# Attention in a macaron block: the softmax row sums of the last four heads taken by matmuls with ones instead of ScalarE's accumulator

## The chip, the core and the metric

The kernel runs on one core of a Trainium2 chip. A core has five engines that run side by side and meet through semaphores: TensorE (PE, matmuls into PSUM), VectorE (DVE), ScalarE (ACT), GpSimd (POOL) and SyncE (SP, which only issues transfers). The metric is the device time of one execution in microseconds (us); a time of a kernel is the median of its runs.

## The reference

The block is a mixture-of-experts layer, an attention layer and the same mixture-of-experts layer again, each added to its input, over x of shape 8 x 1024 x 512 in float32. Only the attention part concerns the change. It has 16 heads of 32 columns:

```python
q = (x @ Wq.T + bq).reshape(B, L, H, hd)      # B, L, H, hd = 8, 1024, 16, 32
k = (x @ Wk.T + bk).reshape(B, L, H, hd)
v = (x @ Wv.T + bv).reshape(B, L, H, hd)
q = _apply_rope(q, cos, sin); k = _apply_rope(k, cos, sin)
scores = jnp.einsum('bqhd,bkhd->bhqk', q, k) / np.sqrt(hd)
attn = jax.nn.softmax(scores, axis=-1)
out = jnp.einsum('bhqk,bkhd->bqhd', attn, v).reshape(B, L, D)
return out @ Wo.T + bo
```

The softmax needs, for every query and head, the maximum of 1024 scores and the sum of their exponentials.

## The kernel before

The work is cut into 32 units: 8 batches b times 4 column blocks c, and a unit holds four heads. The first and the last part of the program are the expert layers; in between, `Attention.run` calls `stage` for every unit and once more at the end. A stage has 16 slots, written out by hand in program order for PE, ACT, DVE and POOL, so no scheduler moves anything: each engine runs its own list in that order, and waits only for data and for free buffers.

A stage does two things at once. It takes a unit's scores for the first time with queries in the rows ("top": matmuls of L1838, 128 queries by 1024 keys for two head pairs in a slot), finds each row's maximum (`tensor_reduce`, L1846, on VectorE), and forms the exponentials of these scores with the accumulator on (L1850, on ScalarE): the exponentials themselves are thrown away, only their sum per row is kept, in `total0` and `total2`. And for the unit before it ("sum") it forms the scores again with keys in the rows: the negative maxima come in as a rank-3 product of bfloat16 pieces (L1802), then the scores (L1809) are added in PSUM, and ScalarE's exponentials (L1816 and L1818) are the weights `pr`. In every even slot `weighed` multiplies the weights of the two slots before with the values (L1906: eight products, which the trace shows as 16 matmul records, of 128 keys by 32 columns for 512 queries; the four heads fill four column strips of the array) and VectorE adds the result to `oT` (L1912 the first time, L1915 later). After four such groups a half of the queries is done, and `oT` is multiplied with the inverse of the sums (L1918, by GpSimd; by VectorE for the very last).

The inverses come from `rows_of`, a small task that starts after each half of a unit's tops: GpSimd splits the maxima in bfloat16 pieces (L1863, L1865), VectorE takes the reciprocals of the sums (L1870, two of 128x8), PE transposes pieces and inverses (L1877, L1880), VectorE copies them out (L1884, L1886), and SyncE writes the inverses to DRAM (L1888) and reads them back spread over 32 partitions a head (L1892) into the tile `d`.

PSUM has eight banks of 512 columns, taken as four pairs with turning roles. In a slot with both parts, pairs b and d hold the sums' scores, a and c the tops'; then b's place becomes the next a, a's the next d, and d's the next b, while c stays c. So PE can write a slot's L1802 into the old a only when the old a has been read for the last time. What an even slot's L1906 or a group of other matmuls needs is put in pair b as soon as it has been read; in the stage without tops it goes to pair c.

Other matmuls fill the slots: projections of the next unit (L1213), values and outputs (L1232). The output of a finished half of a batch is four groups, each a product of four `oT` tiles with the output weights, added to the row x by VectorE (L1946, L1948). The last stage with tops has only one output group, in slots 0 and 1. The stage after it has no tops: it sums the last unit and carries the output of the last batch's first half in its slots 9, 11, 13 and 15. Then `ending` does what is left: the last weighed sums, the output of the second half (L1349, L1360, L1364), the routing of the last tokens to the experts (L272 to L341, among them L296), their ranking, and the scatters into the expert table (L307, by GpSimd), before the second expert layer begins with a gather from that table. `step` hands out the small VectorE tasks of such routing by an estimated credit per slot; `product` hands out small PE tasks where a bank is spare.

Of the kernel before, what the change touches and what calls it, by code (L numbers as in the profile page):

```python
# [13 lines left out]
F32 = mybir.dt.float32  # L14
I32 = mybir.dt.int32
BF16 = mybir.dt.bfloat16
AF = mybir.ActivationFunctionType
ALU = mybir.AluOpType
# [4 lines left out]
P = 128  # L23
NHEAD = 16
HD = 32
# [1029 lines left out]
class Attention:  # L1055
# [13 lines left out]
    def __init__(  # L1069
# [23 lines left out]

        self.passed = 0

    def start(self, task, rank=2):
# [145 lines left out]
    def stage(self, top, sum_, fill, begin, whole=False):  # L1244

        self.loose = []
        for i in range(self.SLOTS):  # L1250
            self.now += 1
            self.scores(i, top, sum_)
            for rank, task in begin.get(i, ()):
                self.start(task, rank)
            b, d, a, c = self.roles
            side = self.pair(b if top and sum_ else d if top else c)
            weigh = i % 2 == 0 and self.behind
            first, second = (side[:, (i + n) % 2, :] for n in range(2))
            self.spare = [first]
            if weigh:  # L1260
                self.spare = []
                self.weighed(first)
            if sum_:
                self.behind.append((*sum_, i, self.prs))
            if self.half:
                assert i not in fill
                self.group(P, 512, second, False)
            elif i in fill:
                self.half = fill[i]()
                if whole:  # L1270
                    self.group(0, 512, second, False)
                else:
                    self.group(0, P, second, bool(weigh))
            if not (top and sum_ or self.half or i in fill):
                self.spare.append(second)
            for _ in list(self.spare):
                self.product()
            self.step(3.0 if not top else 1.2 if i % 2 else 2.0)
            self.roles = [d, a, b, c]
        self.spare = None  # L1280

    def last_sums(self):
        if self.behind:
            self.weighed(self.take())

    def run(self):
        nc, tc = self.nc, self.tc
# [497 lines left out]
    def scores(self, i, top, sum_):  # L1785


        nc, pool = self.nc, self.pool
        heads = [slice(h * HD, (h + 1) * HD) for h in range(4)]
        at_b, at_d, at_a, at_c = self.roles  # L1790
        self.prs = {}
        if sum_:
            q, k = self.qk[sum_][0], self.qk[sum_][1]
            n, t = divmod(i, self.LT)
            row = self.mrow[(*sum_, n)]
            sbs = [(2, self.pair(at_b)), (0, self.pair(at_d))]
            if not top:
                sbs = [(2, self.pair(at_d)), (0, self.pair(at_b))]
            for pair, sb in sbs:
                for h in range(2):  # L1800
                    at = (pair + h) * HD
                    nc.tensor.matmul(  # L1802
                        sb[:, h, :], self.ones16[at : at + 3, :], row[at : at + 3, :],
                        start=True, stop=False,
                    )
            for pair, sb in sbs:
                for h in range(2):
                    at = heads[pair + h]
                    nc.tensor.matmul(  # L1809
                        sb[:, h, :], k[at, t * P : (t + 1) * P], q[at, n * 512 : (n + 1) * 512],  # L1810
                        start=False, stop=True,
                    )
                self.prs[pair] = pr = pool.tile([P, 2, 512], F32, tag="pr", bufs=6, name="pr")
                if pair and top:
                    for h in range(2):
                        nc.scalar.activation(pr[:, h, :], sb[:, h, :], AF.Exp)  # L1816
                else:
                    nc.scalar.activation(pr, sb, AF.Exp)  # L1818
        if top:
            qa, ka = self.qk[top][0], self.qk[top][1]  # L1820
            j, odd = divmod(i, 2)
            g, j = divmod(j, 4)
            assert {(*top, 0, g), (*top, 1, 0), (*top, 1, 1)} <= self.done, (top, i, self.tasks)
            if i % 8 == 0:
                self.held = {
                    name: pool.tile([P, 4, n], F32, tag=name, name=name)
                    for name, n in (("nm", 4), ("total0", 2), ("total2", 2))
                }
                self.until[g] = self.now + 8
            nm, se = self.held["nm"], {pair: self.held[f"total{pair}"] for pair in (0, 2)}  # L1830
            at_q = slice(j * P, (j + 1) * P)
            own, swapped, cross = qa[:, g * 512 : (g + 1) * 512], self.swapped[(*top, g)], self.cross[top]
            tops = [(0, self.pair(at_a)), (2, self.pair(at_c))]
            for pair, sa in tops:
                for m in range(2):
                    at = heads[pair + m]
                    here = m == odd
                    nc.tensor.matmul(  # L1838
                        sa[:, m, :], (own if here else swapped)[at, at_q],
                        ka[at, m * 512 : (m + 1) * 512] if here else cross[at, :],  # L1840
                        start=True, stop=True,
                    )
            for pair, sa in tops:
                h = pair + odd
                flat = sa.rearrange("p m k -> p (m k)")
                nc.vector.tensor_reduce(nm[:, j, h : h + 1], flat, AX.X, ALU.max, negate=True)  # L1846
            for pair, sa in tops:
                h = pair + odd
                flat = sa.rearrange("p m k -> p (m k)")
                nc.scalar.activation(  # L1850
                    flat, flat, AF.Exp, bias=nm[:, j, h : h + 1], accum_out=se[pair][:, j, odd : odd + 1],
                )
            if i % 8 == 7:
                self.start(self.rows_of(*top, g, nm, se), rank=0)

    def rows_of(self, b, c, g, nm, se):


        nc, pool = self.nc, self.pool
        yield WAIT, 1  # L1860
        p, m = self.pieces[g], nm
        for i in range(3):
            nc.gpsimd.tensor_copy(p[:, :, :, i], m)  # L1863
            if i < 2:
                nc.gpsimd.tensor_tensor(nm, m, p[:, :, :, i], ALU.subtract)  # L1865
        yield WAIT, 1
        yield DVE, 0.3
        over = pool.tile([P, 4, 4], F32, tag="sum", name="sum")
        for pair, total in se.items():
            nc.vector.reciprocal(over[:, :, pair : pair + 2], total)  # L1870
        yield WAIT, 1
        yield PE, 0.7

        bank = self.psum.tile([P, 512], F32, name="tp16")
        tp = bank[:, 0:256].bitcast(BF16).rearrange("p (t q) -> p t q", t=4)
        for t in range(4):
            nc.tensor.transpose(  # L1877
                tp[:, t, :], p[:, t, :, :].rearrange("p h d -> p (h d)"), self.ident16
            )
        nc.tensor.transpose(  # L1880
            bank[0:16, 256:384], over.rearrange("p t h -> p (t h)"), self.s.ident
        )
        self.mrow[b, c, g] = row = pool.tile([P, 512], BF16, tag="mrow", name="mrow")
        nc.vector.tensor_copy(row, tp.rearrange("p t q -> p (t q)"))  # L1884
        few = pool.tile([16, P], F32, tag="few", bufs=1, name="few")
        nc.vector.tensor_copy(few, bank[0:16, 256:384])  # L1886
        kept = self.inverse[g]
        nc.sync.dma_start(kept.rearrange("h (t q) -> t h q", q=P), few)  # L1888
        yield WAIT, 8
        self.over[b, c, g] = d = pool.tile([P, 512], F32, tag="d", name="d")  # L1890
        for h in range(4):
            nc.sync.dma_start(  # L1892
                d[h * HD : (h + 1) * HD, :], kept[h : h + 1, :].partition_broadcast(HD)
            )

    def weighed(self, po):


        nc, LT, behind = self.nc, self.LT, self.behind
# [3 lines left out]
        for j, (_, _, _, prs) in enumerate(behind):  # L1903
            for h in range(4):
                at = h * HD
                nc.tensor.matmul(  # L1906
                    po[at : at + HD, :], self.v[b][t + j][:, c * P + at : c * P + at + HD],
                    prs[h // 2 * 2][:, h % 2, :], start=(j == 0), stop=(j == len(behind) - 1),
                )
        if t == 0:  # L1910
            self.oT[b, c, n] = oT = self.pool.tile([P, 512], F32, tag="oT", bufs=10, name="oT")
            nc.vector.tensor_copy(oT, po)  # L1912
            return
# [215 lines left out]
```

## Time and profile before

| | |
|---|---|
| time, median of 3 runs (lowest to highest) | 4379.53 us (4377.94 to 4381.6) |
| the profiled execution's own time | 4387.33 us |
| its span, first to last instruction | 4385.5 us |
| TensorE busy in the span | 4253.2 us (97%), mean granted clock 0.985 |
| ScalarE busy | 2617.3 us (60%) |
| VectorE busy | 2593.8 us (59%) |
| GpSimd busy | 1402.3 us (32%) |

Durations come from the profiled execution, which is one run; its time is compared with the median where a forecast needs it. Matmuls are pipelined and the profile models their ends, so a busy TensorE is not TensorE at its peak. The granted clock is the share of full speed that the throttle gives TensorE. The attention stages lie between 925 and 3590 us of the span; the last stage with tops takes 3441 to 3525 us, the stage without tops 3525 to 3582.

### The profile page before, as it was taken

To read this page: it belongs to the slowest core of one execution; us is meant where nothing else is said; L and a number is where in the kernel's file an instruction comes from. 1 tells how busy PE (TensorE), PEld (TensorE's weight loads), DVE (VectorE), ACT (ScalarE), POOL (GpSimd) and SP (SyncE) were. 2 spreads that over 40 slices of the span, in tenths; PEclk is the share of its full clock that TensorE was granted. 3 is DMA by queue.
4 is the path that set the end of the run, shared out by engine and by line. 5 is a ranking of instruction groups with operands and counts; after the bars stand their busy time and mean duration, and the time that the engine had idled before them with its cause. 6 is when DMAs were issued, how large, how long until landed. Compare 5 with 4: busy or idle time off the path is not lost.

```text
span 4385.5 us, 84431 instructions
## 1 busy us (share of the span) xinstructions
PE 4253.2 (97%) x32371; PEld 2412.4 (55%) x32371; DVE 2593.8 (59%) x4942; ACT 2617.3 (60%) x4325; POOL 1402.3 (32%) x1640
## 2 busy tenths in 40 slices
PE   8899999989999999999999999999999879999999
PEld 6566777744444444444444444444444335667777
DVE  8434433356666876876776877777766634334333
ACT  6112122137888888888888888888888842122221
POOL 7344444321232232232232232332232213333332
PEclk9999999988999999999999999999999999999999
DMA  4656666531112212222212212312212116566664
GB/s 156 221 187 192 211 209 230 182 110 50 43 47 64 80 46 66 77 47 65 80 46 63 80 46 65 81 45 66 79 39 62 35 43 210 185 206 205 215 222 164
DMA packets 310835, 495.59 MB, mean 113 GB/s; under 512 B 65049, under 2 KB 99235, under 8 KB 310418
## 3 DMA queue, kind: packets, MB, share of 16 engines
q1 hardware_dynamic: 269698, 412.06, 30.9%
q0 software_dynamic: 39776, 76.77, 5.4%
q8 instruction: 257, 4.21, 0.4%
q14 instruction: 160, 1.31, 0.1%
q10 hardware_dynamic: 944, 1.23, 0.1%
HBM read 379.85 MB, written 87.93 MB: 107 GB/s over the span
## 4 chain that ended last, share of the span: by engine, by line
PE 90%; DVE 4%; issue 2%; ACT 1%; DMA 1%; POOL 1%; SPq 0%; POOLq 0%; DVEq 0%; ACTq 0%
PE s L1232 11%; PE s L1838 11%; PE s L1213 11%; PE gp L969 10%; PE s L1809 10%; PE s L1906 10%; PE up L969 10%; PE yp L1015 9%; PE s L1802 4%; PE tp L957 2%; PE yp L1023 1%; ACT s L1850 1%; DVE nm L1846 1%; DVE st L164 1%; PE s L207 1%
## 5 line engine op out<-in xcount | busy, mean ns | idle before, releaser
L1846 DVE TENSOR_REDUCE nm<-s 128x1 f32<-128x1024 f32 x1024 | 1205.7, 1219 | 556.2 <-PE s L1838 555.0
L1850 ACT ACTIVATE s<-s,nm 128x1024 f32<-128x1024 f32 x1024 | 1114.3, 1088 | 158.4 <-DVE nm L1846 147.6
L974 ACT ACTIVATE sg<-gp 128x320 f32<-128x320 f32 (+7 forms) x256 | 99.7, 389 | 1062.0 <-PE gp L969 1008.3
L1816 ACT ACTIVATE pr<-s 128x512 f32<-128x512 f32 x992 | 538.3, 594 | 242.6 <-PE s L1809 240.4
L1744 POOL TENSOR_TENSOR raw<-raw,a 128x512 f32<-128x512 f32 x125 | 158.8, 1270 | 1374.0 <-DMA rot<-raw 1202.4
L1838 PE MATMUL s<-cross,swapped 32*128 32x512 f32 x2048 | 569.7, 615 | 7.5 <-DMA cross<-k 3.1
L1838 PE MATMUL s<-k,q 32*128 32x512 f32 x2048 | 567.4, 611 | 0.0
L1818 ACT ACTIVATE pr<-s 128x1024 f32<-128x1024 f32 x528 | 541.9, 1030 | 22.4 <-PE s L1809 22.4
L1809 PE MATMUL s<-q,k 32*128 32x512 f32 x4096 | 551.6, 598 | 0.5 <-issue 0.3
L1213 PE MATMUL s<-hT,wqk 128*32 128x128 f32 (+2 forms) x4864 | 502.1, 323 | 9.1 <-ACT pr L1816 5.2
L1906 PE MATMUL s<-pr,big 128*32 128x512 f32 x4096 | 495.2, 601 | 0.7 <-DVE lg L1948 0.7
L969 PE MATMUL gp<-bT,wg 128*128 128x272 f32 (+7 forms) x1984 | 488.7, 389 | 0.0
L969 PE MATMUL up<-bT,wu 128*128 128x272 f32 (+7 forms) x1984 | 484.9, 387 | 0.0
L1213 PEld LDWEIGHTS s<-hT,wqk 128*32 128x32 f32 (+1 forms) x4864 | 295.5, 127 | 287.7 <-ACT pr L1816 96.9
L1015 PE MATMUL yp<-wd,a 128*128 128x512 f32 x992 | 445.9, 592 | 0.0
L969 PEld LDWEIGHTS gp<-bT,wg 128*128 128x128 f32 x1984 | 371.6, 190 | 87.4 <-issue 21.4
L969 PEld LDWEIGHTS up<-bT,wu 128*128 128x128 f32 x1984 | 374.4, 190 | 70.3
L996 DVE TENSOR_TENSOR a<-sg,up 128x320 f32<-128x320 f32 (+7 forms) x256 | 110.8, 433 | 490.8 <-PE up L969 395.9
L1906 PEld LDWEIGHTS s<-pr,big 128*32 128x32 f32 x4096 | 107.3, 109 | 357.6 <-ACT pr L1816 194.1
L1838 PEld LDWEIGHTS s<-k,q 32*128 32x128 f32 x2048 | 243.8, 186 | 105.2 <-DVE raw L1685 40.2
L1019 DVE SCALAR_TENSOR_TENSOR ys<-yp,gates,x 128x512 f32<-128x512 f32 x128 | 96.1, 751 | 336.9 <-PE yp L1015 336.9
L1838 PEld LDWEIGHTS s<-cross,swapped 32*128 32x128 f32 x2048 | 227.4, 186 | 120.4 <-DVE raw L1685 21.9
(310 smaller groups left out, 5388.7 us busy)
## 6 DMA issues: line engine op xcount, KB each, us to landing
wg<-in_w_gate SPq DMA_DIRECT2D x62, 1024.0 KB
wu<-in_w_up SPq DMA_DIRECT2D x62, 1024.0 KB
wd<-in_w_down SPq DMA_DIRECT2D x62, 1024.0 KB
rot<-raw SPq DMA_DIRECT2D x1000, 32.0 KB
all<-in_x SPq DMA_DIRECT2D x32, 512.0 KB
xt<-first_rows SPq DMA_DIRECT2D x64, 256.0 KB
swapped<-q SPq DMA_DIRECT2D x256, 64.0 KB
d<-inverse SPq DMA_DIRECT2D x256, 64.0 KB
```

The source lines that it names most:

```text
L969: nc.tensor.matmul(acc, w[:, k, f * P : (f + 1) * P], to.bT[:, k, 0:width], start=(k == 0), stop=(k == s.KD - 1),)
L1015: nc.tensor.matmul(yp, a[:, f, i * P : (i + 1) * P], wd[:, f, :], start=(f == 0), stop=(f == KF - 1),)
L1213: self.nc.tensor.matmul(acc[a : a + w, lo:hi], one[:, a : a + w], two[:, lo:hi], start=(i == 0), stop=(i == len(terms) - 1),)
L1232: self.nc.tensor.matmul(bank[a : a + w, 0 : to - at], one[:, a : a + w], two[:, at:to], start=(i == 0), stop=(i == len(terms) - 1),)
L1802: nc.tensor.matmul(sb[:, h, :], self.ones16[at : at + 3, :], row[at : at + 3, :], start=True, stop=False,)
L1809: nc.tensor.matmul(sb[:, h, :], k[at, t * P : (t + 1) * P], q[at, n * 512 : (n + 1) * 512], start=False, stop=True,)
L1816: nc.scalar.activation(pr[:, h, :], sb[:, h, :], AF.Exp)
L1818: nc.scalar.activation(pr, sb, AF.Exp)
L1838: nc.tensor.matmul(sa[:, m, :], (own if here else swapped)[at, at_q], ka[at, m * 512 : (m + 1) * 512] if here else cross[at, :], start=Tru ...
L1846: nc.vector.tensor_reduce(nm[:, j, h : h + 1], flat, AX.X, ALU.max, negate=True)
L1850: nc.scalar.activation(flat, flat, AF.Exp, bias=nm[:, j, h : h + 1], accum_out=se[pair][:, j, odd : odd + 1],)
L1906: nc.tensor.matmul(po[at : at + HD, :], self.v[b][t + j][:, c * P + at : c * P + at + HD], prs[h // 2 * 2][:, h % 2, :], start=(j == 0), s ...
```

## The change

For the units in `self.plain`, which holds only the last one (batch 7, column block 3), the accumulating exponentials are left out. In the stage without tops, every even slot that calls `weighed` for this unit now also multiplies the same weights `pr` with a block of ones, of the same shape as the block of values, into the second bank of the pair, `pd`. Each row of the result holds the sum over 256 keys, already spread over the 32 partitions of its head, so neither transposes nor transfers are needed. VectorE copies or adds `pd` into `d` and, after a half's last group, takes the reciprocal of all of `d` (128x512); these stand in its order ahead of the copy or add into `oT`. `rows_of` then only splits, transposes and copies the maxima. A slot that uses the second bank hands out no small PE task. Everything else is the same.

```diff
@@ __init__
+        self.plain = {(B - 1, s.KD - 1)}
@@ stage
             weigh = i % 2 == 0 and self.behind
+            both = bool(weigh) and self.behind[0][:2] in self.plain
...
-                self.weighed(first)
+                self.weighed(first, second if both else None)
...
-            if not (top and sum_ or self.half or i in fill):
+            if not (top and sum_ or self.half or i in fill or both):
                 self.spare.append(second)
@@ last_sums
-            self.weighed(self.take())
+            both = self.behind[0][:2] in self.plain
+            self.weighed(self.take(), self.take() if both else None)
@@ scores
+            if top in self.plain:
+                se = {}
...
             for pair, sa in tops:
+                if not se:
+                    continue
                 h = pair + odd
                 flat = sa.rearrange("p m k -> p (m k)")
                 nc.scalar.activation(
@@ rows_of
         yield WAIT, 1
+        if not se:
+            yield PE, 0.5
+            bank = self.psum.tile([P, 512], F32, name="tp16")
+            tp = bank[:, 0:256].bitcast(BF16).rearrange("p (t q) -> p t q", t=4)
+            for t in range(4):
+                nc.tensor.transpose(
+                    tp[:, t, :], p[:, t, :, :].rearrange("p h d -> p (h d)"), self.ident16
+                )
+            self.mrow[b, c, g] = row = pool.tile([P, 512], BF16, tag="mrow", name="mrow")
+            nc.vector.tensor_copy(row, tp.rearrange("p t q -> p (t q)"))
+            return
@@ weighed
-    def weighed(self, po):
+    def weighed(self, po, pd=None):
...
+        if pd is not None:
+            for j, (_, _, _, prs) in enumerate(behind):
+                for h in range(4):
+                    at = h * HD
+                    nc.tensor.matmul(
+                        pd[at : at + HD, :], self.s.ones[:, at : at + HD],
+                        prs[h // 2 * 2][:, h % 2, :], start=(j == 0), stop=(j == len(behind) - 1),
+                    )
+            if t == 0:
+                self.over[b, c, n] = self.pool.tile([P, 512], F32, tag="d", name="d")
+                nc.vector.tensor_copy(self.over[b, c, n], pd)
+            else:
+                d = self.over[b, c, n]
+                nc.vector.tensor_tensor(d, d, pd, ALU.add)
+                if t + len(behind) == LT:
+                    nc.vector.reciprocal(d, d)
```

More of the change, by code (lines that the diff above doesn't have):

```diff
@@ L1261, in stage @@
                 self.spare = []
-                self.weighed(first)
+                self.weighed(first, second if both else None)
             if sum_:
                 self.behind.append((*sum_, i, self.prs))
+            assert not (both and (self.half or i in fill))
             if self.half:
```

## The prediction

> **What bounds the kernel now.** I read the page first: the shares of the chain that ended last, and the costliest groups.
>
> ```profile
> PE 90%; DVE 4%; issue 2%; ACT 1%; DMA 1%; POOL 1%; SPq 0%; POOLq 0%; DVEq 0%; ACTq 0%
> L1850 ACT ACTIVATE s<-s,nm 128x1024 f32<-128x1024 f32 x1024 | 1114.3, 1088 | 158.4 <-DVE nm L1846 147.6
> ```
>
> Over the whole run TensorE (PE) sets the end, and ScalarE's accumulating exponentials (L1850) are 1% of the chain. That average hides the one place where the change acts: the last of 32 stages that form row maxima, and the stage behind it that only sums. So I asked for busy times by stretch: one ordinary stage, the part of the last maximum stage that has no projections or outputs left in it (slots 2 to 15), and the start of the sum stage.
>
> ```profile
> 3365.00:3445.00 80.00, 80.00 (x808) 38.22 (x804) 59.02 (x104) 69.65 (x115) 23.53 (x28) 1.00 0.22 58
> 3451.60:3525.40 73.80, 56.01 (x411) 21.64 (x411) 45.86 (x73) 60.39 (x100) 7.35 (x11) 0.91 0.04 12
> 3527.00:3570.00 43.00, 39.74 (x316) 15.64 (x313) 9.12 (x21) 25.48 (x27) 3.70 (x7) 0.98 0.06 19
> ```
>
> Columns are length, then busy PE, weight loads, VectorE (DVE), ScalarE (ACT), GpSimd, then the granted clock. In an ordinary stage PE is never idle, so freed ScalarE time there would be worth nothing. In slots 2 to 15 of the last maximum stage PE idles 18 of 74 us and gets a clock of 0.91; ScalarE is the busiest. The chain of waits shows how a slot turns there, and, below the dots, two slots of the sum stage.
>
> ```profile
> 3467.21 0.39 PE s L1802 x2
> 3467.60 0.86 PE s L1809 x8
> 3468.46 0.87 PE s L1838 x6
> 3469.36 1.24 DVE nm L1846
> ...
> 3470.62 1.21 ACT s L1850 x2
> ...
> 3471.87 0.39 PE s L1802 x2
> ...
> 3544.63 1.85 PE s L1906 x16
> 3546.49 0.33 PE s L1802 x4
> 3546.81 0.94 PE s L1809 x8
> 3547.78 1.03 ACT pr L1818
> ...
> 3548.85 0.39 PE s L1802 x2
> ```
>
> The first part is a loop of 4.66 us per slot: scores, maximum, exponential, and only then may PE write the next scores into that PSUM pair. The second is 5.47 us for two slots: PE works all but about 1.0 us, which it waits for one exponential.
>
> **What the change does, part by part.** The order of instructions after the change holds what the diff says: 32 L1850 and their accumulator reads go, eight groups of 16 matmul records with ones come in right behind the L1906 groups of the sum stage and its end, and VectorE gets eight 128x512 copies or adds and two 128x512 reciprocals. GpSimd's order stays. Ten transfers of inverses leave SP's queue; they are off the chain, worth nothing.
>
> *Gain in slots 2 to 15.* Fourteen turns of 4.66 us are 65.2; the stretch took 73.7 (3451.66 to 3525.39). The other 8.5 are four windows of 3.4 us at half clock (in each a slot's L1809 took 1.71 for 0.86, its L1838 some 0.7 more: 1.5 each, 6.0), one PE halt at 3507.55 (L1809 2.15 for 0.86: 1.3), and VectorE's routing work (about 1.2). Without L1850 the pair is free when its maximum ends. An odd slot then takes 0.39 + 0.86 + 0.87 + 0.03 + 1.24 + 0.04 = 3.45. In an even slot the weighed sums (L1906) come between: PE needs 1.85 + 0.33 + 0.86 + 0.87 = 3.9, but VectorE needs 1.07 from the start of L1838 to its first maximum, 2.35 for the two, 0.69 for the add from PSUM that frees the next bank: 4.1. Seven pairs are 7 x 7.55 = 52.9. VectorE is the next bound: per slot only about 1.1 us of it is free, and the routing lumps (3.0 us in slot 8 to 9, 1.4 in slot 4, others smaller) overflow that by about 3.5 together. Half-rate windows followed PE idleness: the 3.4 us before each were at most 62% busy. Odd slots now idle about 1.1 us of 3.45, so I keep two of four windows (3.0) and the halt (1.3). The stretch is then 52.9 + 3.5 + 3.0 + 1.3 = 60.7, a gain of 13.0. Slots 0 and 1 carry an output group each and are PE-bound; nothing there.
>
> *Loss in the sum stage.* The products with ones have the shape and count of L1906, so 1.86 us each. They stand between an even slot's scores and the odd slot's scores, while PE's 1.0 us wait comes after the odd scores; nothing hides them. Seven in the stage: 13.0. VectorE's copies and adds of the new sums are free where no output group follows, since it is 80% idle there.
>
> *The reciprocal 128x512* is in no row. The rows for its price:
>
> ```profile
> L1870 DVE RECIPROCAL sum<-total 128x8 f32<-128x8 f32 x128 | 16.7, 172 | 0.0
> ...
> L300 DVE RECIPROCAL se<-se 128x4 f32<-128x4 f32 x16 | 2.8, 178 | 0.6
> L1563 DVE RECIPROCAL sd<-rstd 128x4 f32<-128x4 f32 x16 | 2.6, 169 | 0.0
> L510 DVE RECIPROCAL se<-se 128x8 f32<-128x8 f32 x7 | 1.4, 203 | 0.2
> ```
>
> L300 and L510 both run alone after a wait, so their difference is a slope: 25 ns for 4 columns, 6.25 ns a column, 0.18 + 508 x 0.00625 = 3.35 us. L1870 runs pipelined and its 172 ns for 8 columns is no more than 4 columns cost; by that a 128x512 would cost what an add does, 0.66. From L1563 (169) to L510 the step is 34 ns for 4 columns, 8.5 each, 0.17 + 508 x 0.0085 = 4.5. So the ends are 0.66 and 4.5. I take 3.35, since an instruction that waits for its operand, as here, is like L300 and L510.
>
> The Trainium skill speaks against a cheap one: VectorE: DVE Perf Modes (section "First, the fixed hardware budget") says that reciprocal is an iterative divide with a repeat count of 8. If that means 8 cycles a column at the 0.96 GHz of its specifications, one costs an estimated 4.4 us; by the page the sum below would be 2 us worse.
>
> *Where it bites.* (1) Slot 8 ends the first half's sums. Its reciprocal stands in VectorE's queue ahead of the add into oT, and slot 9's output group (L1232) writes the bank which that add frees, so output, later scores and exponentials queue behind it. From the end of the products: 0.07 + 0.69 + 0.05 + 3.35 + 0.05 + 0.69 = 4.9; PE comes to L1232 after 1.1. Stall 3.8. GpSimd's multiply (1.27) ends before the last terms need it. (2) The output groups of slots 11, 13, 15 and the transposes of slot 3 wait for two VectorE operations in place of one: 1.45 against 1.1, 0.35 each, 1.4. (3) The end is one VectorE queue:
>
> ```profile
> 3582.57 1.92 PE L1906 MATMUL s<-pr,big 128*32 128x512 f32 x16 [0.72 <-DVE lg L1948]
> 3585.30 0.66 DVE L1915 TENSOR_TENSOR oT<-oT,s 128x512 f32<-128x512 f32 x1
> ...
> 3586.61 0.37 DVE L296 TENSOR_TENSOR lg<-s,oh 128x128 f32<-128x128 f32 x1
> ```
>
> The last products end at 3584.49 + 1.86 = 3586.35; then add 0.69, reciprocal 3.35, and L1915 ends at 3591.2, not 3585.96: 5.2. Behind it wait routing, ranking, the table's scatters and the second expert phase; VectorE has no pause before 3590, so all 5.2 pass on. Small transposes that go give back 0.1.
>
> **Sum.** Loss 13.0 + 3.8 + 1.4 + 5.2 - 0.1 = 23.3, gain 13.0: 10.3 us slower. The profiled execution took 4387.33 us (its span 4385.5), 7.8 more than the median of the runs, 4379.53; I carry the difference over: 4389.8 us. What a measurement can tell from no change is 0.2%, 8.8 us.
>
> **Rivals.** *A cheap reciprocal* (0.66, as L1870 hints): the stall of slot 9 falls to 1.1 and the end to 2.5, loss 17.9, net +4.9: 4384.4, within 0.2%. For it: L1870. Against: the slope. Chance 0.22. *Not slower: the freed slots run clean.* If no window falls to the 62% that preceded the half-rate ones, and the routing lumps fit VectorE's free time, slots 2 to 15 take 52.9, gain 20.8; this decides once the loss is below that, so it needs the cheap reciprocal too: 17.9, net -2.9, 4376.6. For it: every half-rate window there followed PE idling. Against: VectorE is nearly full. Chance 0.1. *VectorE takes ScalarE's place*: lumps and half clocks stay as they are (52.9 + 3.5 + 7.3, gain 10.0) and each reciprocal costs 4.5 (loss 25.6): +15.6, 4395.1. For it: VectorE is full in every even slot as soon as L1850 goes. Chance 0.2. My forecast keeps 0.48.
>
> **The numbers.** Range 4380 to 4397: it leaves out most of the clean case below and, above, the last rival with a further half-rate window or two after slot 9's stall. Slower by over 0.2% (above 4388.3): about seven in ten of the forecast (0.34), all of the last rival (0.2), a little of the cheap one (0.05): 0.59. Faster by over 0.2% needs 9 us, beyond even the clean case: 0.03. The rest, 0.38, is the same.
>
> **What would show it.** Slots 2 to 15 at about 61 us with VectorE the busiest beside PE, and no wait for L1850; pairs of slots in the sum stage at 7.3 us, not 5.47; one reciprocal row near 3.3 us and L1232 in slot 9 waiting on VectorE for nearly 4; L296 of the end some 5 later behind its L1906. It is wrong if the reciprocal is under 1 us, if the freed stretch is below 56, or if the ones' products take less than L1906's.

## The result, and the profile after

| | before | after |
|---|---|---|
| time, median of 20 runs each (lowest to highest) | 4378.41 us (4375.87 to 4381.6) | 4386.78 us (4381.91 to 4388.46) |
| ratio after to before, 95% interval | | 1.0017 (1.001 to 1.0024) |
| the profiled execution's own time; span | 4387.33; 4385.5 us | 4387.99; 4386.1 us |
| TensorE's mean granted clock | 0.985 | 0.984 |

The change costs 8.4 us (the interval is 4.4 to 10.5 us). New lines push the old ones down: L1802, L1809, L1816, L1818, L1838, L1846, L1850, L1906, L1912, L1915, L1918 and L1232 of before are L1807, L1814, L1821, L1823, L1845, L1853, L1859, L1926, L1948, L1951, L1954 and L1234 after; the products with ones are L1934, the adds of the new sums L1943, the reciprocal L1945.

The page of after, the same two lines as before: 32 of ScalarE's accumulating exponentials are gone, and VectorE's share of the chain has gone from 4% to 3%. At this scale nothing can be read of the change.

```profile
PE 90%; DVE 3%; issue 3%; ACT 1%; DMA 1%; POOL 1%; SPq 0%; POOLq 0%; DVEq 0%; ACTq 0%
L1859 ACT ACTIVATE s<-s,nm 128x1024 f32<-128x1024 f32 x992 | 1079.5, 1088 | 149.3 <-DVE nm L1853 139.3
```

Busy times by stretch of after (length, then PE, weight loads, VectorE, ScalarE, GpSimd, then the granted clock): slots 2 to 15 of the last stage with tops, and slot 0 of the sum stage.

```profile
3445.92:3503.79 57.87, 50.12 (x405) 17.94 (x406) 44.33 (x70) 28.22 (x43) 7.32 (x11) 0.97 0.03 11
3503.79:3506.90 3.11, 3.11 (x32) 0.91 (x35) 1.08 (x1) 1.77 (x2) 0.00 (x0) 1.00 0.00 0
```

The first was 73.80 us. ScalarE's work there is halved (60.39 to 28.22 us), VectorE is the busiest beside PE, as forecast, and the clock is 0.97 instead of 0.91. The second row is one that the forecast had not looked at. In before, with the same 32 matmul records, it is:

```profile
3525.39:3530.14 4.75, 4.75 (x32) 1.16 (x35) 0.00 (x0) 3.01 (x4) 0.00 (x0) 0.64 0.00 0
```

PE is busy all the time in both; only the clock differs, 0.64 against 1.00. That slot cost 1.6 us in before and doesn't after. The chain of waits of after shows how two slots of the sum stage turn now (start, duration, what):

```profile
3514.09 0.33 PE s L1807 x4
...
3515.38 1.03 ACT pr L1823
...
3517.70 1.85 PE s L1926 x16
3519.56 1.72 PE s L1934 x16
3521.28 0.33 PE s L1807 x4
```

From the first line to the last is 7.19 us; it was 5.47. The whole difference is L1934, whose 1.72 us stands in the chain, and the wait for L1823 is as long as it was. The timeline of after shows slots 8 and 9, where a half's sums end (in brackets: how long the engine was idle before, and what ended that):

```profile
3533.75 1.90 PE L1934 MATMUL s<-pr,ones 128*32 128x512 f32 x16
...
3536.44 3.35 DVE L1945 RECIPROCAL d<-d 128x512 f32<-128x512 f32 x1
3539.71 0.63 DVE L1951 TENSOR_TENSOR oT<-oT,s 128x512 f32<-128x512 f32 x1
3540.39 0.61 PE L1234 MATMUL s<-bo,ones 128*128 128x272 bf16 x2 [3.55 <-DVE oT L1951]
3540.80 5.13 PE L1234 MATMUL s<-wvo,oT 128*128 128x272 f32 x16
```

PE stands still for 3.55 us until the add into `oT` (L1951) has emptied the bank, and that add stood behind the reciprocal. The output group after it takes 5.13 us. The same group in before, for which PE doesn't wait:

```profile
3553.32 3.83 PE L1232 MATMUL s<-wvo,oT 128*128 128x272 f32 x16
```

The stall in after is followed by part of a group at half rate: the granted clock is a half from 3540.0 to 3543.4. The timeline's end of after:

```profile
3579.08 1.93 PE L1934 MATMUL s<-pr,ones 128*32 128x512 f32 x16
...
3581.79 3.35 DVE L1945 RECIPROCAL d<-d 128x512 f32<-128x512 f32 x1
3585.06 0.63 DVE L1951 TENSOR_TENSOR oT<-oT,s 128x512 f32<-128x512 f32 x1
...
3586.33 0.37 DVE L296 TENSOR_TENSOR lg<-s,oh 128x128 f32<-128x128 f32 x1
```

L296 starts 8.96 us after the start of the last weighed sums (L1926, at 3577.37); in before it was 4.04 us after them.

To add this up, every profile is cut at the start of the same matmuls: the first score products of the slots, the last weighed sums, and the first matmul of the second expert phase. Behind that every kernel takes 756 to 757 us. Before and after were each run and profiled a second time as experiments (E5 and E6 below), which shows how far a stretch varies by itself.

| us | before | again | after | again |
|---|---|---|---|---|
| slots 2 to 15, last stage with tops | 73.80 | 72.19 | 57.94 | 61.83 |
| sum stage, slot 0 | 4.68 | 4.68 | 3.04 | 3.04 |
| slots 1 to 7 | 17.44 | 17.44 | 22.65 | 22.65 |
| slots 8 and 9 | 9.57 | 9.57 | 16.37 | 17.54 |
| slots 10 to 14 | 19.51 | 19.51 | 25.26 | 25.26 |
| slot 15 to the last weighed sums | 5.98 | 5.98 | 6.25 | 6.25 |
| from there to the expert phase | 45.85 | 45.61 | 51.51 | 51.38 |
| sum | 176.8 | 175.0 | 183.0 | 188.0 |

The first pair of profiles differs by 6.2 us, the second by 13.0, on average 9.6. The medians say 8.4. The two first profiled executions themselves differ by only 0.7 us, because in after slot 2 of the last stage with tops begins 5.7 us earlier (3445.92 against 3451.66), ahead of all that the change touches. In the second profile of the same program it begins at 3455.85, so it isn't the change's doing. The traces say where it arises: from the first weighed sums of the attention to slot 2 it is 2430 us in before, before again and after again, and 2419 in after. Why is open.

### The profile page after: what moved, and what is told of

Same layout as the page of the kernel before. It is cut to its first block, busy times and chain, and to the rows that moved or that the text cites. A ratio compares the mean times of both kernels' runs of the same rounds, so it can differ in the third digit from the quotient of the medians.

```text
span 4386.1 us, 84607 instructions
## 1 busy us (share of the span) xinstructions
PE 4258.2 (97%) x32497; PEld 2414.6 (55%) x32497; DVE 2603.6 (59%) x4946; ACT 2580.2 (59%) x4261; POOL 1400.3 (32%) x1640
## 4 chain that ended last, share of the span: by engine, by line
PE 90%; DVE 3%; issue 3%; ACT 1%; DMA 1%; POOL 1%; SPq 0%; POOLq 0%; DVEq 0%; ACTq 0%
PE s L1215 11%; PE s L1234 11%; PE s L1845 11%; PE gp L969 10%; PE up L969 10%; PE s L1926 10%; PE s L1814 10%; PE yp L1015 9%; PE s L1807 4%; PE tp L957 2%; PE yp L1023 1%; DVE nm L1853 1%; PE s L207 1%; ACT s L1859 1%; DVE st L164 1%
## 5 line engine op out<-in xcount | busy, mean ns | idle before, releaser
L1853 DVE TENSOR_REDUCE nm<-s 128x1 f32<-128x1024 f32 x1024 | 1206.1, 1219 | 547.5 <-PE s L1845 546.4
L1859 ACT ACTIVATE s<-s,nm 128x1024 f32<-128x1024 f32 x992 | 1079.5, 1088 | 149.3 <-DVE nm L1853 139.3
L1821 ACT ACTIVATE pr<-s 128x512 f32<-128x512 f32 x992 | 538.2, 594 | 267.6 <-PE s L1814 266.1
L1845 PE MATMUL s<-cross,swapped 32*128 32x512 f32 x2048 | 564.6, 612 | 5.0 <-DMA cross<-k 3.1
L1823 ACT ACTIVATE pr<-s 128x1024 f32<-128x1024 f32 x528 | 542.0, 1030 | 39.9 <-PE s L1814 39.9
L1845 PE MATMUL s<-k,q 32*128 32x512 f32 x2048 | 564.5, 608 | 0.0
L1814 PE MATMUL s<-q,k 32*128 32x512 f32 x4096 | 541.8, 596 | 0.0
L1926 PE MATMUL s<-pr,big 128*32 128x512 f32 x4096 | 492.8, 599 | 0.7 <-DVE lg L1984 0.7
L1845 PEld LDWEIGHTS s<-k,q 32*128 32x128 f32 x2048 | 243.3, 185 | 104.6 <-DVE raw L1690 39.6
L1926 PEld LDWEIGHTS s<-pr,big 128*32 128x32 f32 x4096 | 106.9, 109 | 351.7 <-ACT pr L1821 191.0
L1845 PEld LDWEIGHTS s<-cross,swapped 32*128 32x128 f32 x2048 | 224.6, 185 | 121.8 <-DVE raw L1690 23.3
```

The lines of the kernel that those rows point to most:

```text
L1814: nc.tensor.matmul(sb[:, h, :], k[at, t * P : (t + 1) * P], q[at, n * 512 : (n + 1) * 512], start=False, stop=True,)
L1845: nc.tensor.matmul(sa[:, m, :], (own if here else swapped)[at, at_q], ka[at, m * 512 : (m + 1) * 512] if here else cross[at, :], start=Tru ...
L1859: nc.scalar.activation(flat, flat, AF.Exp, bias=nm[:, j, h : h + 1], accum_out=se[pair][:, j, odd : odd + 1],)
L1926: nc.tensor.matmul(po[at : at + HD, :], self.v[b][t + j][:, c * P + at : c * P + at + HD], prs[h // 2 * 2][:, h % 2, :], start=(j == 0), s ...
```

## The experiments

The theory is the forecast's: a gain of about 13 us in the last stage with tops, a loss of about 23 us behind it, of which the products' time on PE is 12 to 13 and the two reciprocals ahead of the adds into `oT` are most of the rest. A rival has the products hidden or half hidden once ScalarE's exponentials go, and most of the loss in the reciprocals alone. Another has the 8 us come from elsewhere: a build that differs, not work. The kernels of one set were run on one chip beside before, whose medians were 4392.36 us beside E1 to E4, 4390.75 beside E5 to E7, and 4379.3 beside E8. So each kernel is compared with before by the ratio within its own set. The edits are shown against after, that of E8 against E7; "..." stands for lines left out.

**E1, the gain alone.** The exponentials go, the products do not come. The row sums are left out: `d` is filled with ones by GpSimd.

```diff
-            both = bool(weigh) and self.behind[0][:2] in self.plain
+            both = False
...
+        if (b, c) in self.plain and t == 0:
+            self.over[b, c, n] = self.pool.tile([P, 512], F32, tag="d", name="d")
+            nc.gpsimd.memset(self.over[b, c, n], 1.0)
```

> The last unit's accumulating exponentials go, but no products with ones and no reciprocal come in: the sums are left out, and oT is multiplied with a tile of ones. Theory A (two large sums of opposite sign): slots 2 to 15 of the last stage with maxima take 58 us in place of 74, slot 0 of the next 3.1 in place of 4.75, and the time falls by 15 to 17.5 us against the kernel before, about 4362. Theory B (both sides were mostly hidden): the exponentials stood beside work that lasts as long, and the time falls by at most 4 us.

Measured 4373.44 us, ratio 0.9959 (0.9945 to 0.9972). Its stretches sum to 162.4 us, 13.5 less than the mean of the two profiles of before. Busy times of slots 2 to 15:

```profile
3454.87:3514.02 59.15, 50.33 (x407) 18.01 (x406) 44.31 (x70) 28.22 (x43) 7.32 (x11) 0.97 0.03 10
```

That is after's gain without after's products, and slots 1 to 7 of the sum stage take 17.83 us, within 0.4 of before's 17.44. The gain is there and belongs to the exponentials.

**E2, the loss alone.** Before, with its exponentials and its own way of the inverses, and besides it the products, adds and reciprocals, whose result nobody reads.

```diff
-            if top in self.plain:
-                se = {}
...
-                self.over[b, c, n] = self.pool.tile([P, 512], F32, tag="d", name="d")
-                nc.vector.tensor_copy(self.over[b, c, n], pd)
+                self.unread[b, c, n] = self.pool.tile([P, 512], F32, tag="raw", name="unread")
+                nc.vector.tensor_copy(self.unread[b, c, n], pd)
```

> The kernel before with the 64 products with ones, the copies and adds of their result and the two reciprocals added, in the places where the change puts them; the accumulating exponentials and the inverses' way through DRAM stay and are used, the new result is read by nobody. Theory A: the sum stage and the end take 23 to 24 us more, about 4402. Theory B: PE's waits and idle VectorE take most of it, 8 to 12 us more, about 4388.

Measured 4410.64 us, ratio 1.004 (1.0026 to 1.0053). Its stretches sum to 200.5 us, 24.6 over before's mean. Slots 1 to 7 of the sum stage:

```profile
3534.08:3556.67 22.59, 20.30 (x190) 6.37 (x188) 5.00 (x11) 11.63 (x12) 2.42 (x6) 1.00 0.05 13
```

Slots 2 to 15 take 75.35 us, no less than in before, and slots 1 to 7 are after's (22.65), so the loss doesn't need the exponentials gone, and nothing in the sum stage hides the products. By stretches the halves add: -13.5 + 24.6 = +11.1, and after has +9.6. By medians they don't: -18.9 + 18.3 = -0.6. Each of the two lies 5 to 6 us lower than its stretches say. From E1 to E2 the medians (37.2) and the stretches (38.1) agree, so the misfit lies between these two and before, of which this set has no profile. The set's median of before isn't simply too high, since E3, whose stretches sum to before's, also has before's time. Offsets of this size between two copies of one program are what E5 shows; whether they are the cause here is open.

**E3, no reciprocal.** After without its two reciprocals; `oT` is then multiplied with the sums, not their inverses.

```diff
                 nc.vector.tensor_tensor(d, d, pd, ALU.add)
-                if t + len(behind) == LT:
-                    nc.vector.reciprocal(d, d)
```

> The changed kernel without its two 128x512 reciprocals (oT is multiplied with the sums, not their inverses). Theory A: each 3.35 us stands on the path, one before slot 9's output group and one in VectorE's queue at the end, and the half clock after the stall goes too: 7 to 8 us less than the changed kernel, 4379 to 4380. Theory B: the products alone cost the time and the reciprocals are covered: within 2 us of the changed kernel, 4385 to 4387.

Measured 4390.76 us, ratio 0.9997 (0.9988 to 1.0006). In the sum stage only the stretches with a reciprocal move: slots 8 and 9 take 11.56 us instead of 16.37, the end 48.10 instead of 51.51; all other stretches of the sum stage are after's to 0.01 us. The output group of slot 9, from its timeline:

```profile
3547.32 0.39 PE L1234 MATMUL s<-bo,ones 128*128 128x272 bf16 x2 [0.22 <-DVE oT L1949]
```

The stall is 0.22 us in place of 3.55, and the 16 matmuls after it are back at 3.83 us. The two reciprocals cost 8.2 us by these stretches (4.8 + 3.4), against 6.7 by their own duration; the ratios of after and of E3 (1.0017 and 0.9997, from two sets) put it at 8.8 us.

**E4, the reciprocal behind the add into `oT`.** This asks whether it is the bank that PE waits for, or the inverse.

```diff
-                if t + len(behind) == LT:
-                    nc.vector.reciprocal(d, d)
...
         if t + len(behind) == LT:
+            if pd is not None:
+                nc.vector.reciprocal(self.over[b, c, n], self.over[b, c, n])
```

> The changed kernel with the reciprocal moved behind the add into oT, so that the add frees the bank first. Theory A: slot 9's output group starts about 0.3 us late in place of 3.6, but its last terms then wait about 1.9 us for GpSimd's multiply, which still comes after the reciprocal; the end does not change: 1.3 to 2.7 us less than the changed kernel, 4384 to 4385.5. Theory B (the multiply, not the bank, held the output group): no change in slot 9's end, same time as the changed kernel.

Measured 4397.22 us, ratio 1.0015 (1.0006 to 1.0024), not told apart from after. Slots 8 and 9 take 13.30 us, between after's 16.37 and E3's 11.56: the wait for the bank, with the half clock behind it, was the larger part (3.1 of 4.8 us). What is left is the output's last terms, which need the multiplied `oT` and so the inverse. The group starts after 0.22 us and waits inside for GpSimd's multiply:

```profile
3549.74 0.39 PE L1234 MATMUL s<-bo,ones 128*128 128x272 bf16 x2 [0.22 <-DVE oT L1949]
3554.35 1.18 PE L1234 MATMUL s<-wvo,oT 128*128 128x272 f32 x4 [1.46 <-POOL oT L1954]
```

The end is unchanged at 51.81 us, as it must be where all of it is one VectorE queue.

**E5 and E6, the same two programs again**, in one set, for what two builds of one kernel differ by.

> The kernel before once more, for a second profile of it and for the width of no change. By the stretches of the first profile: slots 2 to 15 take 73.8 us, of which one PE halt of about 2 us at slot 13 may be missing this time (71.5 to 74); the sum stage from slot 1 to the last sums 52.4, the end 45.9. Time against before: 0 within 0.1%.

> The changed kernel once more, on the same chip as the others of this set. Slots 2 to 15 at 58 us, sum stage 70.5, end 51.5; 6 to 9 us more than before. If the sum of the two one-sided kernels (-18.9 and +18.3) were the truth, it would be 0 instead.

Before again: 4395.61 us, ratio 1.0009 (1 to 1.0018). After again: 4400.42, ratio 1.0022 (1.0013 to 1.0031). So 0.1% stands between two copies of one program, and a median alone can't carry a finding of 5 us; after stands above both copies of before, but its interval overlaps that of before again. That after is slower rests on its two ratios together with the stretches. Slots 2 to 15 of after again:

```profile
3455.85:3517.68 61.83, 53.02 (x406) 18.84 (x406) 44.39 (x70) 28.22 (x43) 7.34 (x11) 0.92 0.04 10
```

After again has the same work as after and 3.9 us more, at a clock of 0.92 against 0.97: three windows at half clock (3488.0, 3491.4 and 3508.5) where after has one (3478.6).

**E7, the weights added first.** If the products are what costs, one group per half is enough: VectorE adds the eight key tiles' weights in SBUF, and only the sum of them is multiplied with ones, once per half, in the group that ends the half. The reciprocal reads PSUM, stands behind the add into `oT`, and for the first half is cut in four column pieces, each followed by GpSimd's multiply.

```diff
             if sum_:
                 self.behind.append((*sum_, i, self.prs))
+                self.adding(*self.behind[-1])
...
+            for h in range(4):
+                at = h * HD
+                nc.tensor.matmul(
+                    pd[at : at + HD, :], self.s.ones[:, at : at + HD], self.added[n][:, h, :],
+                    start=True, stop=True,
+                )
...
+                for at in [slice(0, 512)] if n else [slice(k * P, (k + 1) * P) for k in range(4)]:
+                    nc.vector.reciprocal(d[:, at], pd[:, at])
+                    (nc.vector if n else nc.gpsimd).tensor_tensor(
+                        oT[:, at], oT[:, at], d[:, at], ALU.mult
+                    )
```

> The changed kernel, but VectorE, four fifths idle in the sum stage, adds the weights of a half's eight key tiles in SBUF first, so that one product with ones per half (0.86 us) replaces four (1.72 each); the reciprocal reads PSUM behind the add into oT, in four column pieces with their multiplies by GpSimd for the first half. Theory A: the gain of 17.5 stays, the products fall from 13.8 to 1.7, slot 9's stall goes, the end costs 3.4 to 4.5: 8 to 12 us less than before, unless VectorE's 28 adds of 128x1024 (about 1.2 us, 4.8 for two slots of 5.5) hold PE up, for which I take off 2 to 4 of that. Theory B (the loss is not PE's time on the products but the second bank and its waits): no better than the changed kernel.

Measured 4382.38 us, ratio 0.9975 (0.9964 to 0.9985): faster than before and, by intervals that don't meet, than after (1.0022). Slots 1 to 7 are at 17.84 us, as in E1 (17.83; before 17.44), and slots 10 to 14 at 19.51, as in before, though VectorE now does 28 adds. The largest group of these adds by form, 24 of the 28, then the first half's products with ones and slot 9 in the timeline:

```profile
L1972 DVE TENSOR_TENSOR added<-added,pr 128x1024 f32<-128x1024 f32 x24 | 27.8, 1217 | 0.0
```

```profile
3542.04 1.07 PE L1934 MATMUL s<-added,ones 128*32 128x512 f32 x8
3546.62 0.28 PE L1234 MATMUL s<-bo,ones 128*128 128x272 bf16 x1 [2.10 <-DVE d L1948]
```

The adds cost 28 x 1.2 = 34 us of VectorE, and by these stretches all of it is beside other work. What is left in slots 8 and 9 (12.78 us against 9.57) is the one group with ones, 1.0 us, and a new wait of 2.10: the output's second part writes the bank that the reciprocal's pieces (here L1948) still read.

**E8, the same with the sums copied out of PSUM first.**

```diff
+                if not n:
+                    nc.vector.tensor_copy(d, pd)
-                    nc.vector.reciprocal(d[:, at], pd[:, at])
+                    nc.vector.reciprocal(d[:, at], pd[:, at] if n else d[:, at])
```

> As e7, but the first half's sums are copied from PSUM to SBUF (0.69 us) before the four pieces of their reciprocal, since in e7 the second part of slot 9's output group waited 2.1 us for the last piece to leave its bank. Theory A: slots 8 and 9 take 11.0 to 11.5 us in place of 12.8 (9.57 before), all else as in e7: 8 to 11 us less than the kernel before. Theory B (the group then waits as long for GpSimd's multiplies): 12.8 again.

Measured 4370.91 us, ratio 0.998 (0.9971 to 0.9989), not told apart from E7. The wait is gone: slots 8 and 9 take 10.52 us, and the timeline has no idle time ahead of slot 9's group.

```profile
3531.22 0.41 PE L1234 MATMUL s<-bo,ones 128*128 128x272 bf16 x2
```

Half of it comes back in slots 10 to 14 (20.66 for 19.51): PE waits 1.08 us ahead of slot 10's weighed sums for VectorE's adds of the output, which stand in its queue behind the reciprocal's pieces and two adds of weights. By stretches E8 is 9.5 us below before's mean and E7 7.4. Both beat before and after.

## Why the prediction was right, step by step

*The gain.* Forecast 60.7 us for slots 2 to 15. The seven profiles without the exponentials (after twice, E1, E3, E4, E7, E8) have 57.9 to 61.8, on average 59.6; against before's mean of 73.0 that is 13.4 gained, and the forecast had 13.0. Single profiles give 11.2 to 15.1, so the last half microsecond of the agreement is luck. The turn it was made from is in the chain of waits of after:

```profile
3461.44 0.69 PE s L1807 x4
...
3464.00 1.85 PE s L1926 x16
3465.85 0.33 PE s L1807 x4
...
3468.21 0.93 ACT pr L1823
...
3469.18 0.62 PE s L1807 x4
```

This pair of slots takes 7.74 us, of which the first has 4.41; the forecast had 7.55 and 4.1, ahead of VectorE's lumps. (Its terms for an odd slot add to 3.43, not 3.45; that is 0.1 us over the stretch.) The forecast let VectorE's maximum alone free the next scores. In the trace PE waits first for ScalarE's weights (L1823, done at 3469.13), and half of L1807 then waits for the first maximum (done at 3469.35; it starts at 3469.41). So the maximum does end the wait, but ScalarE is only 0.2 to 0.3 us behind as the next bound, which the forecast did not see. Of the forecast's two half-clock windows after kept one and after again three, which is most of the spread of 4 us.

*A term that was missed, for the change.* Slot 0 of the sum stage ran at a clock of 0.64 in before: PE had waited 2.40 us for L1850 just ahead of it, in a window in which it was 30% busy. With the exponentials gone PE waits 1.31 us for L1853 there, the window is 62% busy, no half clock follows, and the slot takes 3.04 us, not 4.68. The forecast stopped its gain at the stage's end, 1.6 us too early.

*A term that was missed, against it.* After the stall in slot 9 the output group takes 1.3 us more (5.13 for 3.83). The forecast put half-rate windows after that stall only in its upper end. That the two misses nearly cancel is luck.

*The products.* Forecast 7 x 1.86 = 13.0 us in the chain; measured 1.72 each, 12.0. L1926 comes behind scores, of another shape of weights (32*128 in the trace), and takes 1.85; L1934 comes behind L1926, of its own shape (128*32), and takes 1.72. That the change of shape is the 0.13 is read off the order, not tested. "Nothing hides them" held: E2 shows the same slots 1 to 7 with the exponentials kept.

*The reciprocal.* The term with the widest ends, 0.66 to 4.5, and the value taken, 3.35, from the slope between two small rows that ran alone. The groups by form of after:

```profile
L1945 DVE RECIPROCAL d<-d 128x512 f32<-128x512 f32 x2 | 6.7, 3353 | 0.1
```

3353 ns. That refutes the cheap reciprocal and the 4.5. That 3.35 was hit to the last digit is luck: the slope came from 25 ns over 4 columns, and the small rows do not lie on the line of the larger ones (by 895 ns for 128 columns and 3350 for 512, eight columns would take 0.13 us, and took 0.20). The Trainium skill's repeat count of 8 (VectorE: DVE Perf Modes, section "First, the fixed hardware budget"), read as 8 cycles a column, gave an estimate of 4.4 us; the measurement decides, and it is a quarter lower.

*Where it bites.* The stall in slot 9 was 3.55 us for 3.8, on the wait that was named, and E4 shows that the bank is most of it. The three output groups of slots 11, 13 and 15 waited 0.28, 0.22 and 0.22 us, not 0.35 each (slots 10 to 14 take 25.26 - 19.51 = 5.75 us more, of which three products are 5.16), and the transposes of slot 3 cost next to nothing (slots 1 to 7 take 5.21 more, of which three products are 5.16). The end lost 5.7 us for 5.2; in E1, whose end does the same work as before's, it is 47.3, 1.5 longer than before's, so the last half microsecond of it is within what the end varies by.

*The sum.* Forecast +10.3; the medians +8.4; the stretches +6.2 and +13.0. The loss behind slot 0 was forecast at 23.3 and is 23.7 and 25.0 by the two pairs of profiles; the gain, slot 0 with it, is 17.5 and 12.0 for 13.0. The forecast held a change of over 0.2% more likely (0.59) than one that can't be told from none (0.38). The ratio, 1.0017, is on the less likely side, so the range and the mechanism held and this choice did not. The rival with clean slots is out: 59.6, not 52.9, and it needed the cheap reciprocal. The rival in which VectorE takes ScalarE's place is out on both its conditions: the gain is 13.4, not 10.0, and the reciprocal isn't 4.5. The rival of a gain that doesn't come or a loss that is hidden is refuted by E1 and E2 in their stretches.

What stays open: why two builds of a kernel differ by 0.1%, why the place where slot 2 begins varies by 12 us between profiles (3445.80 in E8, 3457.71 in E7), and with it why the medians of E1 and E2 don't add up as their stretches do.

## What to carry to other kernels

Work that is moved from an engine with slack to the one that sets the end is paid in full unless that engine has a wait into which it fits: the exponentials were worth 13 us in the one stage whose turn they set (in an ordinary stage, where PE is never idle, leaving them out was not tried), and the products cost 12 us where PE waits 1 us in two slots. Look for the engine that is free in the stage the work moves to: VectorE was 80% idle there, and where it adds the weights first and leaves PE one group of products in four (E7, E8), +0.2% becomes -0.2%. A long instruction on a short queue belongs behind whatever frees a buffer for the bottleneck (in E4 that is 3.1 us by the stretches, too little for the medians to show), and if it is cut in pieces, look which bank the pieces hold meanwhile.

## What the runs showed of the hardware that was not expected

A reciprocal costs VectorE per column what about five adds do: 3353 ns for 128x512 in float32, and in E7 and E8 895 ns in the median for a 128x128, so (3350 - 895) / 384 = 6.4 ns a column, against 0.69 us for a 128x512 add from PSUM.

The granted clock falls to a half, for one window of 3.4 us at a time, after some windows in which PE was little busy. In slots 2 to 15 of the last stage with tops and in the sum stage's slots, in the profiles of before and after, the windows just ahead of such ones were 30 to 62% busy in PE (in after's slot 9 stall 7%), and windows of 65% and more were never followed by one. Windows of 51, 62 and 63% weren't followed either, so the busy share alone doesn't decide it. Behind these slots even the 65% does not hold: in after, PE is busy all the time from 3581.0 to 3584.4, mostly with L1354's products of 32 columns, and half clock follows.

So a stall costs twice, once as idle time and once as half-rate work behind it: the 3.55 us of slot 9 cost the output group behind it another 1.3 in after, 1.2 in E2 (5.06 us) and 2.5 in after again (6.30 us).

Counted from the end of the group before, 16 product records behind scores take 1.85 us, and 16 behind a group of their own shape 1.72.
